# Two attention layers on one core: the rows of an image to come are transposed and measured one pass earlier and kept in DRAM

## The chip, the cores and the metric

The kernel runs on one core of a Trainium2 chip (the NeuronCore has TensorE for matrix products, VectorE, ScalarE and GpSimd for elementwise work, and SyncE, here called SP, which issues most DMAs). The metric is the time of one execution on the device in microseconds; lower is better. In the profile the engines are called PE (TensorE products), PEld (TensorE weight loads), DVE (VectorE), ACT (ScalarE), POOL (GpSimd) and SP.

## What is computed

x is 8 images of 32 x 32 positions with 512 channels, all float32. Two layers follow one another, each added to its input. Both first take a group norm over 32 groups of 16 channels.

```python
# layer 0: 16 heads of 32
x = x + L0(gn(x))     # qkv = xn @ w_qkv; softmax(q k^T * 32**-0.5) v; @ w_proj + b_proj
# layer 1: 4 heads of 128, with relative position logits
x = x + L1(gn(x))     # scores = (xn @ Wq * 128**-0.5) k^T + pos(q); softmax(scores) v; @ Wo

def _gn(v, G=32, eps=1e-5):
    g = v.reshape(B, H, W, G, C // G)
    m = mean(g, axis=(1, 2, 4)); s = var(g, axis=(1, 2, 4))
    return (g - m) / sqrt(s + eps)
```

`pos(q)` is a sum of a term by columns and a term by rows of the image; both come from products of q with two small tables.

## The kernel before

**Data.** An image is 1024 rows (positions) of 512 channels. The kernel works on it turned over, channels on the 128 partitions in CC = 4 chunks, 1024 positions along a row, so that one image is one "block" of 128 x 4 x 1024 float32 (2 MB). There are BLOCKS = 8 such blocks in SBUF. A projection is done as seven products of quarter matrices in place of eight (`seven`, L461; the sums that this needs are formed on VectorE by `forming`, L397, the operations at L424: four additions or subtractions of 128 x 1024, of which the second is wanted by the second product of a unit, and the last, called s4, by the sixth). The seven products of a unit run in the order 0, 5, 1, 4, 6, 2, 3 into three PSUM banks called x, y and z in the profile; products 5, 4 and 2 go to y. After product 5 VectorE makes a = y + p1 (L475), after product 4 b = y + p1 (L483), and the next product into y has to wait for that read.

**Passes.** The main loop (L1481) goes over b = 0 to 8. Pass b runs, on PE, the first attention of image b (`attention_0`, L766). Between its steps `side_by_side` (L1395) puts the rest of the work, in this order: the output projection of the first attention of image b-1 (`after_0`), the output projection of the second attention of image b-2 (`after_1`) woven with the second group norm of image b-1 (`norm_1`, `sums_1`), the projections of the second layer of image b-1 (`second`), the second attention of image b-1 (`attention_1`, L961), and the three projections of the first layer of image b+1 (`before_0`). The second attention counts nothing in that planning, so that all its steps stand together: it is a stage of its own of some 110 to 125 us. Images 0 and 1 are loaded in other ways; from image 2 on `load_apart` does it.

**First attention.** A step computes scores for four heads of 32 (L779), one exponential of 128 x 2048 on ScalarE (L794, tile e_room), four products with the values (L805), and one addition of 128 x 2048 on VectorE (L817, e_room) for the sum of the softmax. There are three e_room buffers, one of which holds the sum, and a single scores tile in PSUM. So an addition that is late holds up the exponential two steps later, and that the next scores.

**Second attention.** 64 steps (4 heads, 2 halves of the queries, 8 tiles of the keys). For each step SP loads a tile of 128 x 512 position rows (pos<-pr, 256 KB, L943), one of 8 slots; GpSimd adds the columns' term to it (L948), some four steps ahead; ScalarE copies it into PSUM (L957); PE adds the scores to it (L998); ScalarE takes the exponential (L1001); PE multiplies with the values (L1012); VectorE adds up e (L1026, L1028). A new slot is loaded when the copy has read it.

**The load of an image (`load_apart`, L1122).** It is woven into the second attention (L1545), three calls in every eight steps. For each of 8 parts (chunk cc, half h) `load_blocks` (L289) issues four DMAs of 64 KB on SP into a tile xs of tag "row", in pieces of 32 channels (128 B), up to three parts ahead. VectorE turns xs over into the block (L1135), `statistics` (L299) takes bn_stats of both halves of a chunk (L306) and an aggregate (L307), and SP puts the chunk away to DRAM (`put_away`, L275) for the addition of the residual later. Then `group_norm` (L312) runs: some ten small VectorE operations on 32 columns, a reciprocal root on GpSimd (rstd, L350, held behind the newest of GpSimd's position additions), four tensor_scalar of 128 x 1024 that write the block in place (L354), and the sums of `forming`.

**Tag "row".** Three buffers of 128 x 512. xs tiles use them, and so do the tiles ot of `put_out` (L1344), into which VectorE turns the output over before four DMAs of 64 KB bring it out (L1355).

**Weights.** `Stream` (L199) loads each weight tile (L235, L231) seven products ahead into one of 16 buffers, all on SP. In the second attention it holds back seven loads and releases one per step from step 6 on (L1072).

**What sets the order.** The kernel is written against a framework that schedules each engine's instructions from their dependencies and buffers and may move an instruction ahead of earlier ones of the program; `tc.issue_after(x)` keeps an instruction behind x. Each engine and SP's queue then runs its instructions strictly in the order given. A DMA on SP that waits (for a transpose, or a free buffer) holds up all DMAs behind it.

Of the kernel before, what the change touches and what calls it, by code (L numbers as in the profile page):

```python
# [27 lines left out]
def quick_path(  # L28
# [260 lines left out]
    def load_blocks(b, cc, h):  # L289

        xs = mem.tile([P, NB // 32, 32], F32, tag="row", name=f"xs_{b}_{cc}_{h}", bufs=3)
        for a in range(P // 32):
            nc.sync.dma_start(
                xs[32 * a : 32 * a + 32],
                by_blocks(xf[b, h * NB : (h + 1) * NB, :], cc * P + 32 * a),
            )
        return xs.rearrange("p t i -> p (t i)")

    def statistics(st, xT, cc, name):  # L299

        if "mv" not in st:
            st["mv"] = mvs[0]
            mvs.reverse()
        s = small.tile([P, NH, 6], F32, tag="st", name=f"st_{name}_{cc}", bufs=2)
        for h in range(NH):
            nc.vector.bn_stats(s[:, h, :], xT[cc][:, h * NB : (h + 1) * NB])  # L306
        nc.vector.bn_aggr(  # L307
            st["mv"][:, : 2 * CC].rearrange("p (s c) -> p c s", c=CC)[:, cc, :],
            s.rearrange("p h s -> p (h s)"),
        )  # L310

    def group_norm(st, xT, name, after=None, behind=None, out=None, apart=False):  # L312
# [33 lines left out]
        if apart:  # L346
            yield 0
        rstd = small.tile([P, CC], F32, tag="rstd", name=f"rstd_{name}")
        with tc.issue_after(spread[0].ins) if apart else nullcontext():
            nc.gpsimd.tensor_tensor(rstd, var, neg_half, op=ALU.pow)  # L350
        yield 0
        for cc in range(CC):
            with tc.issue_after(behind().ins) if behind is not None else nullcontext():
# [11 lines left out]

    in_place = [False]
    behind_sums = [False]
    spread = [None]

    begun = [None]  # L370
    half_done = [None]
# [513 lines left out]
    class Seeds:  # L885
# [59 lines left out]
        def add_up(self, upto):  # L945
            while self.summed < min(upto + 1, H1 * NH * NT):
                i = self.summed
                spread[0] = nc.gpsimd.tensor_tensor(  # L948
                    self.rows[i], self.rows[i], self.columns[i // NT], op=ALU.add
                )  # L950
                self.summed += 1
# [9 lines left out]
    def attention_1(q, k, v, seeds, b, beside=0, final=False):  # L961
# [93 lines left out]
        for i, at in enumerate(steps):  # L1055
            for t in range(i, i + 1 if i < beside else i + 2):
                prepare(t)
            e = front(i, *at)
            for t in range(i + 2, i + 1 if i < beside else i + AHEAD):
                prepare(t)  # L1060
            if pending is not None:
                back(*pending)
            pending = (*at, e)
            for part in ending:
                next(part, None)
            if "ended" in state:
                ending = [finish(*state.pop("ended"))]
                next(ending[0], None)
            if i + 1 < beside:
                prepare(i + 1)  # L1070
            if i > 5:
                stream.release()  # L1072
            stream.behind = seeds.last
            yield 0
# [14 lines left out]
    def load(b, st):  # L1089
# [2 lines left out]
        parts = [(cc, h) for cc in range(CC) for h in range(NH)]  # L1092

        if b > 1:
            yield from load_apart(b, st, parts)
# [23 lines left out]
        for _ in range(2):  # L1119
            yield next(sums)  # L1120

    def load_apart(b, st, parts):  # L1122

        def bring(i):
            with tc.issue_after(stream.behind.ins):
                return load_blocks(b, *parts[i])

        ahead = [bring(i) for i in range(3)]
        yield 0
        x = block(f"x0T_{b}")  # L1130
        xT = chunks(x)
        st["kept"] = []
        for i, (cc, h) in enumerate(parts):
            with tc.issue_after(added[0].ins):
                nc.vector.transpose(xT[cc][:, h * NB : (h + 1) * NB], ahead.pop(0))  # L1135
            if h == NH - 1:
                statistics(st, xT, cc, f"0_{b}")
                st["kept"] += put_away(xT[cc : cc + 1], f"0_{b}_{cc}")
            yield 0
            if i + 3 < len(parts):  # L1140
                ahead.append(bring(i + 3))
        late, later_on = lambda: added[0], lambda: begun[0]
        yield from group_norm(st, xT, f"0_{b}", after=late, behind=late, apart=True)
        fs = st["xn"] = []
        sums = st["sums0"] = forming(x, f"xn0_{b}", behind=(late, late, late, later_on), into=fs)
        for _ in range(3):
            yield next(sums)
# [268 lines left out]
    def chain(*parts):  # L1416
        for part in parts:
            yield from part
# [11 lines left out]
    def later(part, *args):  # L1430

        yield from part(*args)
# [48 lines left out]
    for b in range(B + 1):  # L1481
# [14 lines left out]
        if last is not None:  # L1496
# [21 lines left out]
                total += PRODUCT // 2  # L1518
            rest.append(later(second, b - 1, last))
            total += SECOND  # L1520
            if past is not None and coming is not None:

                total -= 1
# [18 lines left out]
            if here is None:  # L1542
                incoming = later(late_output, past)
            if here is not None and coming is not None:
                rest.append(woven(attention, incoming, 3, 8, (0, 3, 4)))  # L1545
            else:
                rest.append(woven(attention, incoming, 4, 5))
        else:
# [509 lines left out]
```

## Time and profile before

Three runs took 3718.1, 3721.3 and 3730.5 us.

| | |
|---|---|
| median of the runs | 3721.3 us |
| time of the profiled execution | 3727.5 us |
| span of its instructions | 3725.6 us |
| mean granted TensorE clock | 0.995 |
| second attentions with a load beside them (six) | 122.6, 120.0, 119.4, 122.1, 118.5, 123.8 us |
| second attention of the last image (nothing loaded beside it) | 109.5 us |
| 8 transposes and 8 bn_stats of a load | 703 and 690 ns each |
| an xs DMA (64 KB) from issue to landing | 1.9 / 3.8 / 10.2 us (least, median, most) |
| a fetch of 512 KB in whole rows (x1T<-d) | 6.0 us (median) |
| DMA over the span | 419.4 MB, 113 GB/s |

Times are in us unless ns is written. In a line of a group the number after "x" is the count, then come the busy time, the mean of one in ns, and the idle time of the engine before them with what ended it. In the timeline the columns are start, duration, engine, line, operation, what is written and read, the count, and in square brackets the idle time before with its releaser. In a table of windows each engine's column is its busy time in that window. A wait line gives the total, the number of times and the longest.

### The profile page before, as it was taken

The page shows a single profiled execution, that of the slowest core. Times are in us where ns is not written, and L with a number is a line of the kernel's source. Part 1 is how long each engine was busy: PE and PEld are TensorE (multiplying, and loading weights), DVE is VectorE, ACT ScalarE, POOL GpSimd, SP SyncE. Part 2 cuts the span into 40 slices and gives each one's busy share as a digit, 9 for nine tenths or more (in the row PEclk, how much of TensorE's full clock was granted, in tenths as well). Part 3 has the DMA queues.
Part 4 walks back from the last instruction along what each step waited for, and adds up shares of the span by engine and source line. Part 5 has one row for each costly group of instructions (what it writes and reads, how often), then busy time and mean ns, then how long its engine had stood idle before and what let it go on. Part 6 is the DMA issues. An engine that isn't in the chain of part 4 may idle for free.

```text
span 3725.6 us, 81264 instructions
## 1 busy us (share of the span) xinstructions
PE 3657.9 (98%) x33992; PEld 1241.7 (33%) x33998; DVE 2571.9 (69%) x2905; ACT 2000.7 (54%) x2281; POOL 1295.9 (35%) x833
## 2 busy tenths in 40 slices
PE   9999999999999999999999999999999999999998
PEld 4232243222433234332333323333233332333343
DVE  6778667686675856769567695766857669567546
ACT  2555655546554465544655446554565545656254
POOL 1342146131551315513164131731327213166255
PEclk9999999999999999999999999999999999999999
DMA  5122175142842327423383333723337233334376
GB/s 182 62 84 92 41 179 145 48 119 56 189 138 87 89 63 193 120 95 89 80 192 96 94 89 99 190 79 100 85 96 197 73 99 78 93 105 146 93 201 144
DMA packets 575159, 419.41 MB, mean 113 GB/s; under 512 B 279840, under 2 KB 471616, under 8 KB 573760
## 3 DMA queue, kind: packets, MB, share of 16 engines
q1 hardware_dynamic: 563152, 398.33, 40.0%
q0 software_dynamic: 2608, 13.70, 1.0%
q8 instruction: 270, 4.42, 0.5%
q10 hardware_dynamic: 9024, 2.10, 0.3%
q14 instruction: 105, 0.86, 0.1%
HBM read 321.72 MB, written 92.27 MB: 111 GB/s over the span
## 4 chain that ended last, share of the span: by engine, by line
PE 90%; DMA 3%; DVE 2%; POOL 2%; ACT 1%; issue 1%; SPq 0%; ACTq 0%; DVEq 0%; POOLq 0%
PE ps L779 14%; PE acc L805 13%; PE ps L998 10%; PE acc L1012 9%; PE y_v L385 5%; PE y_q L385 4%; PE y_k L385 4%; PE x_v L385 3%; PE z_v L385 3%; PE z_q L385 3%; PE x_k L385 3%; PE x_q L385 3%; DMA pos<-pr 3%; PE z_k L385 3%; PE y_wp L385 2%; PE y_wo L385 2%
## 5 line engine op out<-in xcount | busy, mean ns | idle before, releaser
L817 DVE TENSOR_TENSOR e_room<-e_room 128x2048 f32<-128x2048 f32 x448 | 1077.6, 2405 | 446.4 <-ACT e_room L794 444.6
L794 ACT ACTIVATE e_room<-ps 128x2048 f32<-128x2048 f32 x512 | 961.9, 1879 | 745.2 <-PE ps L779 708.3
L948 POOL TENSOR_TENSOR pos<-pos,columns 128x512 f32<-128x512 f32 x448 | 655.8, 1486 | 246.5 <-DMA pos<-pr 245.4
L779 PE MATMUL ps<-q,k 32*64 32x512 f32 x8192 | 592.5, 613 | 1.0 <-ACT e_room L794 1.0
L998 PE MATMUL ps<-q,k 128*128 128x512 f32 x1024 | 538.6, 609 | 22.9 <-ACT ps L957 22.1
L1012 PE MATMUL acc<-e,v 128*128 128x512 f32 x1024 | 529.5, 600 | 17.9 <-ACT e L1001 17.9
L805 PE MATMUL acc<-e_room,v 128*32 128x512 f32 x4096 | 546.8, 604 | 0.1
L1001 ACT ACTIVATE e<-ps 128x512 f32<-128x512 f32 x512 | 305.5, 597 | 318.7 <-PE ps L998 278.9
L1028 DVE TENSOR_TENSOR es<-es,e 128x512 f32<-128x512 f32 x384 | 277.5, 723 | 194.8 <-ACT e L1001 186.7
L957 ACT COPY ps<-pos 128x512 f32<-128x512 f32 x448 | 264.7, 592 | 82.9 <-POOL pos L948 70.7
L760 POOL TENSOR_TENSOR q<-q,su 128x512 f32<-128x512 f32 x64 | 106.7, 1667 | 554.2 <-DVE su L756 550.6
L1012 PEld LDWEIGHTS acc<-e,v 128*128 128x128 f32 x1024 | 192.8, 191 | 274.0 <-issue 140.8
L998 PEld LDWEIGHTS ps<-q,k 128*128 128x128 f32 x1024 | 185.0, 191 | 269.5 <-issue 175.7
L779 PEld LDWEIGHTS ps<-q,k 32*64 32x64 f32 x8192 | 122.9, 129 | 390.3 <-issue 211.7
L805 PEld LDWEIGHTS acc<-e_room,v 128*32 128x32 f32 x4096 | 81.4, 108 | 411.2 <-issue 363.3
L644 POOL TENSOR_TENSOR k<-b_k,p_k 128x512 f32<-128x512 f32 x32 | 48.0, 1499 | 479.3 <-ACT p_k L489 479.2
L644 POOL TENSOR_TENSOR q<-b_q,p_q 128x512 f32<-128x512 f32 x32 | 60.2, 1882 | 348.4 <-ACT p_q L489 333.9
L644 POOL TENSOR_TENSOR v<-b_v,p_v 128x512 f32<-128x512 f32 x32 | 55.5, 1734 | 352.5 <-ACT p_v L489 349.6
L877 ACT COPY pos<-pp 32x512 f32<-32x512 f32 x128 | 104.2, 814 | 29.2 <-PE pp L868 28.0
L721 DVE STREAM_TRANSPOSE tu<-su 128x512 f32<-128x512 f32 x64 | 45.2, 706 | 89.0 <-ACT su L719 88.9
L1026 DVE TENSOR_TENSOR es<-e,e 128x512 f32<-128x512 f32 x64 | 69.0, 1078 | 41.8 <-ACT e L1001 41.8
L385 PE MATMUL y_q<-f_xn,w_q 128*32 128x512 f32 x768 | 91.3, 593 | 0.8 <-DVE a_q L475 0.6
(228 smaller groups left out, 4572.3 us busy)
## 6 DMA issues: line engine op xcount, KB each, us to landing
pos<-pr SPq DMA_DIRECT2D x448, 256.0 KB, 3.9
w_qkv<-ws_qkv SPq DMA_DIRECT2D x168, 128.0 KB, 2.7
d<-x0T SPq DMA_DIRECT2D x32, 512.0 KB, 4.4
x1T<-d SPq DMA_DIRECT2D x32, 512.0 KB, 6.0
d<-x1T SPq DMA_DIRECT2D x32, 512.0 KB, 3.6
pc<-pos SPq DMA_DIRECT2D x32, 512.0 KB, 6.5
pr<-pos SPq DMA_DIRECT2D x32, 512.0 KB, 7.8
columns<-pc SPq DMA_DIRECT2D x64, 256.0 KB, 5.2
```

The source lines that it names most:

```text
L385: ins = nc.tensor.matmul(out[columns, :], weights[:, columns], moving, start=start, stop=stop, skip_group_check=open_sum,)
L644: nc.gpsimd.tensor_tensor(self.dst[1][1], s(b), s(p7), op=ALU.add)
L779: nc.tensor.matmul(ps[some, r, :], k[m][rows, j * P + 64 * i : j * P + 64 * i + 64], q[m][rows, h * NB : (h + 1) * NB], start=True, stop=True,
L794: exps[0] = nc.scalar.activation(e, ps, AF.Exp, scale=D0 ** -0.5)
L805: nc.tensor.matmul(acc[r * D0 : (r + 1) * D0, :], v[:, j, c0 : c0 + D0], e[:, r, :], start=(j == blocks[0]), stop=(j == blocks[-1]),)
L817: summed[0] = nc.vector.tensor_add(state["esum"], state["esum"], e)
L948: spread[0] = nc.gpsimd.tensor_tensor(self.rows[i], self.rows[i], self.columns[i // NT], op=ALU.add)
L957: self.copied = nc.scalar.copy(ps, rows)
L998: scored[0] = nc.tensor.matmul(ps, k[h][:, keys], q[:, h, queries], start=False, stop=True, skip_group_check=True)
L1001: exps[0] = nc.scalar.activation(e, ps, AF.Exp, scale=1.0 / math.sqrt(D1))
L1012: nc.tensor.matmul(acc, v[:, j, h * D1 : (h + 1) * D1], e, start=(j == 0), stop=(j == NT - 1),)
L1028: added[0] = nc.vector.tensor_add(state["esum"], state["esum"], e)
```

## The change

The work of `load_apart` is divided into two. `turn_ahead(b + 1)` is new. It is woven into the work of pass b ahead of the second attention (that is, beside the first attention of image b), one of its ten calls every six steps of that work. It loads the parts as before, one part ahead, but turns each over into another tile of tag "row" (xt), takes bn_stats of it, and lets SP put that half away to DRAM (256 KB, so eight stores and not four). After the eighth part it runs the small operations of the group norm and the reciprocal root. Its transposes have no `issue_after`, so that dependencies and the three buffers alone say where they stand.

`load_apart`, still beside the second attention, now takes a free block, loads its four chunks from DRAM (512 KB each, whole rows of 4 KB), norms them in place with the mean and rstd that are ready, and forms the sums. The reciprocal root is no longer held behind GpSimd's position additions. The held weights are released from step 33 on and not from step 6, and `load_apart` is called twice in every eight steps and not three times. `statistics` is now a loop over `look_at`; for the other images it does the same operations, chunk by chunk, with one buffer for a chunk's bn_stats and not two.

```diff
     def statistics(st, xT, cc, name):
 
+        for h in range(NH):
+            look_at(st, xT[cc][:, h * NB : (h + 1) * NB], cc, h, name)
+
+    def look_at(st, half, cc, h, name):
+
         if "mv" not in st:
             st["mv"] = mvs[0]
             mvs.reverse()
-        s = small.tile([P, NH, 6], F32, tag="st", name=f"st_{name}_{cc}", bufs=2)
-        for h in range(NH):
-            nc.vector.bn_stats(s[:, h, :], xT[cc][:, h * NB : (h + 1) * NB])
+        if h == 0:
+            st["st"] = small.tile([P, NH, 6], F32, tag=f"st{name[0]}", name=f"st_{name}_{cc}", bufs=1)
+        s = st["st"]
+        nc.vector.bn_stats(s[:, h, :], half)
+        if h < NH - 1:
+            return
         nc.vector.bn_aggr(
...
         rstd = small.tile([P, CC], F32, tag="rstd", name=f"rstd_{name}")
-        with tc.issue_after(spread[0].ins) if apart else nullcontext():
-            nc.gpsimd.tensor_tensor(rstd, var, neg_half, op=ALU.pow)
+        nc.gpsimd.tensor_tensor(rstd, var, neg_half, op=ALU.pow)
...
-            if i > 5:
+            if i > 4 * NT:
                 stream.release()
...
-    def load_apart(b, st, parts):
-
-        def bring(i):
+    def turn_ahead(b, st):
+
+        parts = [(cc, h) for cc in range(CC) for h in range(NH)]
+        ahead = [load_blocks(b, *parts[0])]
+        st["kept"] = [
+            dram.tile([P, N], F32, tag="kept", name=f"d_0_{b}_{cc}", bufs=4 * CC) for cc in range(CC)
+        ]
+        for i, (cc, h) in enumerate(parts):
+            if i + 1 < len(parts):
+                ahead.append(load_blocks(b, *parts[i + 1]))
+            t = mem.tile([P, NB], F32, tag="row", name=f"xt_{b}_{cc}_{h}", bufs=3)
+            nc.vector.transpose(t, ahead.pop(0))
+            look_at(st, t, cc, h, f"0_{b}")
+            nc.sync.dma_start(st["kept"][cc][:, h * NB : (h + 1) * NB], t)
+            yield 0
+        st["x0"] = []
+        st["norm0"] = group_norm(st, st["x0"], f"0_{b}", behind=lambda: added[0], apart=True)
+        for _ in range(2):
+            yield next(st["norm0"])
+
+    def load_apart(b, st):
+
+        x = block(f"x0T_{b}")
+        st["x0"].extend(chunks(x))
+        for kept, xT in zip(st["kept"], st["x0"]):
             with tc.issue_after(stream.behind.ins):
-                return load_blocks(b, *parts[i])
-
-        ahead = [bring(i) for i in range(3)]
-        yield 0
-        x = block(f"x0T_{b}")
-        xT = chunks(x)
-        st["kept"] = []
-        for i, (cc, h) in enumerate(parts):
-            with tc.issue_after(added[0].ins):
-                nc.vector.transpose(xT[cc][:, h * NB : (h + 1) * NB], ahead.pop(0))
-            if h == NH - 1:
-                statistics(st, xT, cc, f"0_{b}")
-                st["kept"] += put_away(xT[cc : cc + 1], f"0_{b}_{cc}")
+                nc.sync.dma_start(xT, kept)
             yield 0
-            if i + 3 < len(parts):
-                ahead.append(bring(i + 3))
+        yield from st.pop("norm0")
         late, later_on = lambda: added[0], lambda: begun[0]
-        yield from group_norm(st, xT, f"0_{b}", after=late, behind=late, apart=True)
         fs = st["xn"] = []
...
             rest.append(later(second, b - 1, last))
             total += SECOND
+            if coming is not None:
+                rest = [woven(chain(*rest), later(turn_ahead, b + 1, coming), 3, 6)]
...
-                rest.append(woven(attention, incoming, 3, 8, (0, 3, 4)))
+                rest.append(woven(attention, incoming, 3, 8, (0, 4)))
```

More of the change, by code (lines that the diff above doesn't have):

```diff
@@ L367, in quick_path @@
     behind_sums = [False]
-    spread = [None]
     begun = [None]
@@ L947, in add_up @@
                 i = self.summed
-                spread[0] = nc.gpsimd.tensor_tensor(
+                nc.gpsimd.tensor_tensor(
                     self.rows[i], self.rows[i], self.columns[i // NT], op=ALU.add
@@ L1094, in load @@
         if b > 1:
-            yield from load_apart(b, st, parts)
+            yield from load_apart(b, st)
             return
```

## The prediction

> **What bounds the kernel now.** First the page: busy time and the chain that ended last.
>
> ```profile
> PE 3657.9 (98%) x33992; PEld 1241.7 (33%) x33998; DVE 2571.9 (69%) x2905; ACT 2000.7 (54%) x2281; POOL 1295.9 (35%) x833
> ...
> PE 90%; DMA 3%; DVE 2%; POOL 2%; ACT 1%; issue 1%; SPq 0%; ACTq 0%; DVEq 0%; POOLq 0%
> ```
>
> TensorE is the bound, so only its own stalls can be won. Second, what PE waited for:
>
> ```profile
> PE ps L998 <- ACT ps L957: 22.1, 22, 2.3
> PE acc L1012 <- ACT e L1001: 17.9, 9, 3.0
> ```
>
> 40.0 us (22 and 9 times, longest 2.3 and 3.0), all in the second attention. Third, the eight second attentions, each window cut from its first score matmul to its last (columns: width, PE, PEld, DVE, ACT, POOL busy, granted clock, DMA share, GB/s; the one at 3280 shares PE with a first attention and is left out):
>
> ```profile
> 510.17:632.75 122.58, 114.65 (x273) 49.05 (x273) 87.45 (x140) 71.96 (x132) 81.18 (x59) 0.99 0.75 185
> 973.19:1093.18 119.99, 114.16 (x274) 49.34 (x274) 91.04 (x142) 72.27 (x133) 84.99 (x61) 0.99 0.74 189
> 1428.68:1548.03 119.35, 113.32 (x275) 48.45 (x275) 89.62 (x142) 72.38 (x133) 85.19 (x61) 1.00 0.73 190
> 1883.53:2005.61 122.08, 114.73 (x274) 49.23 (x274) 90.45 (x142) 72.34 (x133) 85.96 (x61) 0.99 0.74 185
> 2341.11:2459.60 118.49, 112.58 (x275) 48.60 (x274) 90.92 (x142) 72.03 (x133) 85.06 (x61) 1.00 0.75 191
> 2795.10:2918.85 123.75, 116.55 (x276) 49.73 (x275) 89.93 (x142) 72.39 (x133) 83.21 (x61) 0.97 0.70 183
> 3576.21:3685.69 109.48, 109.48 (x269) 49.28 (x266) 68.06 (x113) 71.41 (x132) 79.00 (x61) 1.00 0.84 219
> ```
>
> The first six load the next x beside themselves. The last does not, and never stalls, though it moves more (219 GB/s). The six sum to 726.2 us; six of 109.5 are 656.9; each of the six also holds about 0.88 us of first-attention matmuls. So 726.2 - 656.9 - 5.3 = **64 us** is what the loading costs.
>
> Fourth, inside 2795: VectorE stood for the reciprocal root that GpSimd had behind its additions, and PE behind VectorE.
>
> ```profile
> 2864.57 1.75 DVE L354 TENSOR_SCALAR x0T<-x0T,back,rstd 128x1024 f32<-128x1024 f32 x1 [4.40 <-POOL rstd L350]
> ```
> ```profile
> 2863.02 1.13 PE L998 MATMUL ps<-q,k 128*128 128x512 f32 x2 [1.12 <-ACT ps L957]
> ...
> 2868.74 2.07 PE L1012 MATMUL acc<-e,v 128*128 128x512 f32 x2 [2.88 <-ACT e L1001]
> ```
>
> The same place (steps 40 to 44 of 64) loses 2.7 to 6.5 us in each of the six, 28 us in all. The rest is lost earlier, while 32 xs loads and 4 stores stand between the position rows on SP.
>
> [...] 64 KB of xs (128 B pieces) land in 3.8 us, 256 KB of position rows in 3.9. [...] the window at 2795 has a mean clock of 0.97, and 0.67 between 2865 and 2875, after the 2.88 us stall.
>
> **The change part by part.**
>
> *Leaves the six attentions:* 32 xs issues of 0.49 us on SP (2.1 MB in 128 B pieces), 4 stores of 0.5 MB that wait on SP for statistics, 8 transposes (0.70) and 8 bn_stats (0.69), 4 aggregates (0.21), the chain of nine small VectorE operations (2.5), the reciprocal root (1.0 here) and the wait for it. *Comes:* 4 loads of 0.5 MB in whole rows. They stand at SP between position rows of steps 3 to 17, need a block that the last values product freed, and are wanted from 33 us into the window; fetches of this size landed in 6.0 us. The window then moves 22.6 - 2.1 = 20.5 MB, in larger pieces, where the last window moved 24.0 (219 GB/s x 109.5 us) with no stall. Seven weight loads (0.54 us of SP each) go from step 6 on to step 33 on; PE wants them after step 64, some 50 us later. Value: nearly all of the 64. I leave 0.5 us per window for the four large loads: **-61**. Bounds: all 64; or only the norm's place, 28.
>
> *Added to the first attention:* nothing holds the new transposes back but three row buffers, so the scheduler puts them early: three halves of image b+2 already in pass b, the other five around the query projection of the next pass. There VectorE is full:
>
> ```profile
> 1760.62 2.24 DVE L817 TENSOR_TENSOR e_room<-e_room 128x2048 f32<-128x2048 f32 x1
> 1762.79 0.67 DVE L475 TENSOR_TENSOR a_q<-y_q,p_q 128x512 f32<-128x512 f32 x1
> 1763.39 2.27 DVE L817 TENSOR_TENSOR e_room<-e_room 128x2048 f32<-128x2048 f32 x1
> 1766.51 2.29 DVE L817 TENSOR_TENSOR e_room<-e_room 128x2048 f32<-128x2048 f32 x1 [0.85 <-ACT e_room L794]
> 1768.72 0.69 DVE L483 TENSOR_TENSOR b_q<-y_q,p_q 128x512 f32<-128x512 f32 x1
> 1769.32 1.22 DVE L424 TENSOR_TENSOR f_xn<-x1T,f_xn 128x1024 f32<-128x1024 f32 x1
> ```
> ```profile
> 1770.78 1.90 PE L385 MATMUL y_q<-f_xn,w_q 128*32 128x512 f32 x16
> ```
>
> Passes 2 to 6: one half with its aggregate (1.6 us) goes in at 1745, the next (1.4) between the additions of 1763 and 1766. Delay at 1766: 1.6 - 0.85 idle + 1.4 = 2.1. The last sum f_xn then ends at 1770.5 + 2.1 = 1772.6, and the product that reads it, at 1770.78, starts 1.9 late. Behind it VectorE has idle time (56 of 100 us busy from 1770), which takes the other halves and the small chain. 5 x 1.9 = **+9.5**. Bounds: 0 to 3 us each (two halves and their aggregate all exposed, with nothing below zero: no work leaves this stretch).
>
> Pass 1 has no output stage, and its order packs five halves and the chain into 356 to 381, then three halves of the next image:
>
> ```profile
> 374.47 4.67 DVE L817 TENSOR_TENSOR e_room<-e_room 128x2048 f32<-128x2048 f32 x2
> ...
> 381.39 4.68 DVE L817 TENSOR_TENSOR e_room<-e_room 128x2048 f32<-128x2048 f32 x2
> 385.99 0.68 DVE L475 TENSOR_TENSOR a_q<-y_q,p_q 128x512 f32<-128x512 f32 x1
> ```
> ```profile
> 386.73 1.92 PE L385 MATMUL y_q<-f_xn,w_q 128*32 128x512 f32 x16
> ```
>
> Ahead of that a_q stand 1.6 + 1.4 + 1.6 + 1.4 + 0.7 (halves), 3.4 (the last half with its chain and aggregate) less some 0.5 idle: 9.6 us. It frees the bank that the product at 386.73 writes, so it ends at 396.3 and PE waits 9.6. With a landing that is awaited or a half clock after so long a stall: **+11.5** (6 to 14). In pass 0 three halves of 1.5 meet little slack: **+1** (0 to 4). At the start the statistics now go chunk by chunk, and the second half's copy is awaited one bn_stats earlier: **+1**.
>
> *SP there:* per image 32 xs issues, 8 stores instead of 4, each waiting for its transpose with the weights queued behind it. In pass 3 the unit that PE begins at 1776 has its third weight issued at 1747; now it follows the outputs (to 1764), four xs (2 us) and a store that waits till about 1769: out near 1770, landed 2.4 later, wanted at 1781.7. 9 us to spare: nothing; if that cover fails, PE waits for every weight behind it. The outputs' row buffers, three before, are now two at times; their transposes come as the 2 us landings end: nothing. GpSimd's reciprocal root (1 to 2 us) moves to where GpSimd has some 14 of 100 us busy: nothing. Four matmuls (0.88 us) move from inside each attention to after it: nothing.
>
> Sum: -61 + 9.5 + 11.5 + 1 + 1 = **-38**. The profiled execution took 3727.5 (span 3725.6); 3727.5 - 38 = 3689.5. The median of the three is 6.2 lower, 3721.3: **3683**.
>
> **The rivals.** *A, VectorE's slack hides the moved work* (additions up to 5 us late are borne today): loss about 3, so 3721 - 61 + 3 = 3663. Against: product and last sum are 0.25 us apart at 1770. 0.15. *B, the position stream stays late*: 512 KB loads among rows wanted every 1.7 us; only the norm's 28 is won, 23 is lost: 3716. Against: the last window. 0.14. *C, slower: the three row buffers.* VectorE stands for an xs group whose issue waited on SP for a store, which waited for VectorE: a group issued late costs 4 x 0.49 + 3.8 = 5.8 us. It decides from 38/48 = 0.8 us at each of the 48 halves; with 1.5 more, 48 x 1.5 = 72: 3755. Against: each group is issued some 5 us ahead of its transpose in the order. 0.08. The order was read from the built program, so that the work moves at all is not in doubt.
>
> **How the numbers follow.** Forecast 0.63 (own range 3670 to 3702). Measurement of this kernel tells 0.3%, 11 us, from no change. Faster: forecast, A and a third of B, 0.83; same: the rest of B, 0.09; slower: C, 0.08. The range 3661 to 3713 takes in A, the bounds of the terms and half of B.
>
> **What would show it.** Six attention windows of 109.5 to 111 us with no PE wait over 1 us; a PE wait of about 2 us for f_xn in the query product of passes 2 to 6, one or more summing to some 10 in pass 1; rstd gone from the attention. Wrong if PE there still waits for ACT ps behind POOL pos, or if VectorE waits for xs.

## The result, and the profile after

| | before | changed |
|---|---|---|
| median of six runs each, us | 3725.4 | 3689.3 |
| lowest and highest | 3718.1, 3730.5 | 3688.1, 3691.0 |
| profiled execution: time, span | 3727.5, 3725.6 | 3691.0, 3688.8 |

The ratio is 0.9905, with a 95% interval of 0.9892 to 0.9917: 36 us faster, where 38 were forecast. The median of before in these six runs is 4.1 us above that of the three shown ahead of the prediction. How much is won depends on the occasion: e6 below, which runs as the changed kernel does, was 30 us faster than the runs of before beside it.

Busy time and the chain that ended last, of the changed kernel:

```profile
PE 3641.0 (99%) x33992; PEld 1244.9 (34%) x33998; DVE 2547.7 (69%) x2905; ACT 1999.0 (54%) x2281; POOL 1288.6 (35%) x833
...
PE 94%; DVE 3%; DMA 1%; issue 1%; ACT 1%; POOL 0%; SPq 0%; ACTq 0%; DVEq 0%; POOLq 0%
```

TensorE is still the bound, and the share of the chain that lies on it rose from 90 to 94%. What PE waited for in the changed kernel (total, times, longest):

```profile
PE y_q L391 <- DVE f_xn L430: 9.3, 5, 2.9
PE y_q L391 <- DVE a_q L481: 5.4, 2, 4.8
PE turned L1182 <- DMA x_rows<-in_x: 5.2, 2, 5.0
PE x_v L391 <- issue: 5.0, 1, 5.0
PE y_k L391 <- DVE a_k L481: 2.4, 1, 2.4
PE sums L833 <- DVE e_room L823: 2.1, 2, 1.7
...
PE ps L1004 <- ACT ps L963: 0.5, 2, 0.3
```

The 40 us of waits for ps and e in the second attention are down to 0.5. In their place stand waits for VectorE in the projections: 9.3 us for f_xn, in five places, and 7.8 for a_q and a_k. The six second attentions with a load, and below them the last one without (width, busy time of PE, PEld, DVE, ACT and POOL, clock, DMA share, GB/s):

```profile
524.80:634.30 109.50, 109.50 (x267) 49.28 (x267) 71.66 (x112) 71.44 (x132) 76.97 (x58) 1.00 0.65 187
980.60:1090.00 109.40, 109.40 (x265) 49.23 (x266) 73.07 (x113) 71.88 (x133) 82.06 (x60) 1.00 0.63 188
1428.20:1537.70 109.50, 109.50 (x269) 49.28 (x266) 75.36 (x113) 71.95 (x133) 81.63 (x60) 1.00 0.61 187
1875.70:1985.20 109.50, 109.50 (x268) 49.28 (x266) 73.94 (x113) 71.94 (x133) 82.81 (x60) 1.00 0.63 188
2324.00:2433.50 109.50, 109.50 (x267) 49.29 (x267) 73.11 (x113) 71.92 (x133) 83.39 (x60) 1.00 0.59 187
2771.50:2881.00 109.50, 109.50 (x267) 49.29 (x267) 76.06 (x113) 71.92 (x133) 82.53 (x60) 1.00 0.63 187
3539.30:3648.80 109.50, 109.50 (x270) 49.29 (x267) 68.31 (x113) 71.46 (x132) 79.81 (x61) 1.00 0.89 219
```

All seven have one width to 0.1 us, with PE busy from end to end. Four loads in whole rows cost an attention nothing that can be seen.

**The ledger.** PE runs the same products in both kernels, and in the same order but for a few matmuls of the first attention that left each second attention (eight records in most windows), so each product of one trace can be set against the same product of the other. The shift of its start (changed minus before) says where time was won and lost:

```
                                  shift at its end   step
start (first 50 us)                     +2.4         +2.4
pass 0 (near 100)                       +4.3         +1.9
pass 1 (360 to 396)                    +14.6        +10.3
attention near 550                      +2.5        -12.1
pass 2 (near 860)                       +7.4         +4.8
attention near 1030                     -2.3         -9.6
pass 3 (near 1310)                      -0.5         +1.8
attention near 1490                     -9.5         -9.0
pass 4 (near 1765)                      -7.8         +1.6
attention near 1940                    -19.6        -11.7
pass 5 (near 2220)                     -17.1         +2.4
attention near 2400                    -25.3         -8.2
pass 6 (near 2670)                     -23.6         +1.7
attention near 2850                    -37.0        -13.4
end                                    -36.9
```

The attentions sum to -64.0, the losses to +27.0 (each step is rounded).

### The profile page after: what moved, and what is told of

Read it like the earlier page. It is cut to its first block, busy times and chain, and to the rows that moved or that the text cites. A ratio compares the mean times of both kernels' runs of the same rounds, so it can differ in the third digit from the quotient of the medians.

```text
span 3688.8 us, 81250 instructions
## 1 busy us (share of the span) xinstructions
PE 3641.0 (99%) x33992; PEld 1244.9 (34%) x33998; DVE 2547.7 (69%) x2905; ACT 1999.0 (54%) x2281; POOL 1288.6 (35%) x833
## 4 chain that ended last, share of the span: by engine, by line
PE 94%; DVE 3%; DMA 1%; issue 1%; ACT 1%; POOL 0%; SPq 0%; ACTq 0%; DVEq 0%; POOLq 0%
PE ps L785 14%; PE acc L811 13%; PE ps L1004 12%; PE acc L1018 12%; PE y_v L391 5%; PE y_k L391 4%; PE y_q L391 4%; PE x_v L391 3%; PE z_v L391 3%; PE x_k L391 3%; PE z_k L391 3%; PE z_q L391 3%; PE x_q L391 3%; PE y_wp L391 2%; PE y_wo L391 2%; PE sums L833 2%
## 5 line engine op out<-in xcount | busy, mean ns | idle before, releaser
L954 POOL TENSOR_TENSOR pos<-pos,columns 128x512 f32<-128x512 f32 x448 | 642.7, 1452 | 193.0 <-DMA pos<-pr 190.4
L1004 PE MATMUL ps<-q,k 128*128 128x512 f32 x1024 | 530.2, 600 | 0.5 <-ACT ps L963 0.5
```

The costliest lines, as they stand in the source:

```text
L954: nc.gpsimd.tensor_tensor(self.rows[i], self.rows[i], self.columns[i // NT], op=ALU.add)
L1004: scored[0] = nc.tensor.matmul(ps, k[h][:, keys], q[:, h, queries], start=False, stop=True, skip_group_check=True)
```

## The experiments

Medians in us. The kernel before had medians from 3719.4 to 3727.7 on different occasions, so each kernel's ratio to the runs of before beside it is given too. Where a smaller difference is at stake, the shift of PE between two traces is used.

| run | median | before beside it | ratio, 95% interval |
|---|---|---|---|
| e1, norm later (from before) | 3701.2 | 3727.4 | 0.9931, 0.9914 to 0.9947 |
| e2, xs in one DMA of whole rows (from before) | 3667.3 | 3727.4 | 0.9842, 0.9826 to 0.9859 |
| e3, root held again (from the change) | 3689.2 | 3727.4 | 0.9905, 0.9888 to 0.9921 |
| e4, weights released early (from the change) | 3688.4 | 3727.4 | 0.9895, 0.9879 to 0.9912 |
| e5, halves moved behind the query projection (from the change) | 3664.7 | 3719.4 | 0.9853, 0.9839 to 0.9868 |
| e6, statistics buffers (from the change) | 3689.2 | 3719.4 | 0.9923, 0.9910 to 0.9935 |
| e7, second bn_stats (from the change) | 3710.9 | 3719.4 | 0.9978, 0.9971 to 0.9984 |
| e8, e5 and e6 | 3665.4 | 3719.4 | 0.9855, 0.9840 to 0.9870 |
| e9, xs in four DMAs of whole rows (from before) | 3675.1 | 3727.7 | 0.9860, 0.9844 to 0.9877 |
| e10, pieces of 128 B beside the attention (from the change) | 3696.4 | 3727.7 | 0.9918, 0.9902 to 0.9935 |
| e11, stores later (from before) | 3706.3 | 3724.0 | 0.9945, 0.9928 to 0.9961 |

Two questions are asked of them. What made the 64 us in the attentions (e1 to e4, e9 to e11)? And what made the 27 us of losses (e5 to e8)? They are told in the order of these questions.

### e1: the norm reached five additions later

```diff
         yield 0
+        if apart:
+            yield 0
+            yield 0
         for cc in range(CC):
             with tc.issue_after(behind().ins) ...:
```

> The kernel before, with one edit: the four tensor_scalar of the norm beside the second attention are called two calls later, so VectorE reaches the first of them five additions (about 8.5 us) after the place where it stood for the reciprocal root. GpSimd's order is untouched. My theory (two causes: 28 us lie at the norm's place, steps 40 to 44, because VectorE stands behind GpSimd; 36 us lie earlier and come from the xs loads and stores among the position rows on SP): the waits of PE for e in that stretch go, the waits for ps earlier stay; 20 to 28 us less than the kernel before. Rival (everything comes from late position rows, and PE waits for them there in any case): within 5 us of the kernel before, with the PE waits of steps 40 to 44 now put down to ps behind GpSimd.

Measured: 26 us less. The six windows sum to 702.3 us, 24 less than before. PE's waits in it:

```profile
PE ps L1001 <- ACT ps L960: 23.5, 24, 2.5
...
PE acc L1015 <- ACT e L1004: 2.4, 6, 0.5
```

The wait for e fell from 17.9 to 2.4 us, and the wait for ps stayed (22.1 before). VectorE no longer waits for rstd beside the attention (19.5 us in seven places before). So what the norm's place cost was VectorE standing for GpSimd. The 20 to 28 us of my theory hold, at least as what can be had by this edit alone.

### e2 and e9: the xs parts in whole rows

e2 replaces the four DMAs of a part by one, e9 keeps four:

```diff
-                return load_blocks(b, *parts[i])
+                cc, h = parts[i]
+                xs = mem.tile([P, NB], F32, tag="row", ..., bufs=3)
+                for a in range(0, P, 32):                       # e9
+                    at = (cc * NH + h) * P + a
+                    nc.sync.dma_start(xs[a : a + 32], xf[b, at : at + 32, :])
+                return xs
```

> The kernel before, but beside the second attention each xs part is fetched by one DMA of 256 KB in whole rows of 2 KB from another place of x (the gathering of channels is left out, so other numbers are transposed and normed), in place of four DMAs of 64 KB in pieces of 128 B. Transposes, statistics, stores and the norm stay. My theory: SP spends 8 issues in place of 32 and the rows come on time; of the 36 us that lie ahead of the norm most goes, 20 to 36 us less; what stays is the wait for the reciprocal root, some of it shorter if GpSimd is no longer late. Rival (the four stores that wait on SP for statistics hold the rows up, not the xs loads): less than 10 us less.

> The kernel before, each xs part again by four DMAs of 64 KB on SP as it has them, but each of 32 whole rows of 2 KB from another place of x (the gathering of channels is left out, other numbers are transposed and normed). The run with one DMA of 256 KB in whole rows took back 60 of the 64 us; two things differ there from the kernel before, the number of issues and the size of the pieces. If the pieces of 128 B are the cause: 3665 to 3673, as with one DMA. If the 24 issues more on SP are (24 x 0.49 = 12 us of SP in each window): 3705 or more, within 20 us of the kernel before.

Measured: e2 60 us less, e9 53 us less. e2 was off my range on the good side: I had given whole rows 20 to 36 us and the norm's place the rest, but with whole rows the norm's wait went as well, although the edit touches neither VectorE's nor GpSimd's part of it. e9 took 2 us more than the upper end of what was expected of the pieces. It shows that the number of issues is a small part (8 us between e2 and e9): most of the gain comes from cutting the same 64 KB into rows of 2 KB and not into pieces of 128 B.

It is not that small pieces land late. In this stage a DMA of 64 KB lands 4.1 us after its issue in pieces of 128 B (median of 192, before) and 3.8 in whole rows (e9), and the position rows of the six windows land after 4.5 us on the mean in both. What differs is SP's time.

How 128 B pieces become stalls can be followed there. In the kernel before, part of one window:

```profile
2843.39 2.22 SPq L275 DMA_DIRECT2D d<-x0T  x1
2845.71 1.37 SPq L943 DMA_DIRECT2D pos<-pr  x2
2847.13 0.62 SPq L943 DMA_DIRECT2D columns<-pc  x1
2847.84 1.16 SPq L943 DMA_DIRECT2D pos<-pr  x2
2853.59 0.33 SPq L275 DMA_DIRECT2D d<-x0T  x1
2854.01 3.84 SPq L943 DMA_DIRECT2D pos<-pr  x6
```

The columns are start and duration of SP's issues. SP's issue of a store took 2.22 us, and from 2849.0 to 2853.6 SP stood for the next store, whose chunk VectorE turned over only by 2853.56. Behind it waited position rows, which then left six in a row. The same place of e9, where SP's order is the same:

```profile
2798.60 0.34 SPq L275 DMA_DIRECT2D d<-x0T  x1
2799.05 1.46 SPq L943 DMA_DIRECT2D pos<-pr  x2
2800.56 0.61 SPq L943 DMA_DIRECT2D columns<-pc  x1
2801.26 1.16 SPq L943 DMA_DIRECT2D pos<-pr  x2
2804.75 0.33 SPq L275 DMA_DIRECT2D d<-x0T  x1
2805.17 4.05 SPq L943 DMA_DIRECT2D pos<-pr  x6
```

The store's issue takes 0.34 us, and SP stands 2.3 us and not 4.6. Over the whole of this attention, the sixth, the 32 xs issues take 13.5 us of SP in e9 and 18.8 before, the four stores 1.4 and 5.5. Those 9.4 us are SP's, in a stretch in which every position row waits for SP.

### e3: the reciprocal root held behind GpSimd's additions again

```diff
-        for _ in range(2):
-            yield next(st["norm0"])
+        yield next(st["norm0"])
...
-        nc.gpsimd.tensor_tensor(rstd, var, neg_half, op=ALU.pow)
+        with tc.issue_after(spread[0].ins) if apart else nullcontext():
+            nc.gpsimd.tensor_tensor(rstd, var, neg_half, op=ALU.pow)
```

> The changed kernel, but the reciprocal root is again computed beside the second attention and held behind the newest of GpSimd's position additions, as the kernel before had it; all else as changed. My theory: with the position rows on time GpSimd is ahead when the root is wanted, so little comes back, 0 to 6 us over the changed kernel in the sum of the six attentions; the 28 us of the kernel before were the product of both, a late GpSimd and a VectorE standing behind it. Rival (the hold itself costs what it cost before, wherever it stands): 15 to 28 us more than the changed kernel.

Measured: no difference, and all six windows are 109.5 us. The root that cost up to 26 us before costs nothing where the position rows are on time. The rival falls. In e2 and e9, too, VectorE does not wait for the root beside the attention, though the norm is untouched there. So the wait for the root was a consequence: GpSimd was late because its rows were.

### e4: the held weights released from step 6

```diff
-            if i > 4 * NT:
+            if i > 5:
                 stream.release()
```

> The changed kernel, but the seven held weight loads are again released from step 6 of the second attention on. My theory: seven issues of 0.54 us on SP, spread over seven steps of 1.7 us each, stand between the position rows where the four large loads stand too; 0 to 1 us in each of the six attentions, 0 to 6 us in all. Rival (the later release is what made the position stream come on time): 20 us or more of the gain is lost.

Measured: no difference; the six windows are 109.5 us here too. The later release adds nothing to the gain.

### e10: the pieces of 128 B put back into the attention

```diff
-        for kept, xT in zip(st["kept"], st["x0"]):
-            with tc.issue_after(stream.behind.ins):
-                nc.sync.dma_start(xT, kept)
-            yield 0
+        for cc, xT in enumerate(st["x0"]):
+            for h in range(NH):
+                half = xT[:, h * NB : (h + 1) * NB].rearrange("p (t i) -> p t i", i=32)
+                rows = xf[b, h * NB : (h + 1) * NB, :]
+                for a in range(P // 32):
+                    with tc.issue_after(stream.behind.ins):
+                        nc.sync.dma_start(half[32 * a : 32 * a + 32], by_blocks(rows, cc * P + 32 * a))
+                yield 0
```

> The changed kernel, but the four loads of the second attention come from x itself in 32 DMAs of 64 KB in pieces of 128 B straight into the block, and not from DRAM in whole rows (the turning over is left out there, so the normed numbers are others; everything ahead of the attention stays, no row buffer, transpose, statistics or store is in the attention). If the pieces of 128 B beside the position rows cost the time: the six attentions lose 20 to 60 us again in their sum. If it was what SP waited for (a free row buffer, a store behind VectorE): within 5 us of the changed kernel.

Measured: 3696.4, 7 us more than the changed kernel, so between the two forecasts and near the second. The profiled execution took 3691.2 us; the other three took 3696 to 3698. Two windows of the profile:

```profile
1875.90:1986.60 110.70, 110.70 (x277) 49.42 (x274) 76.50 (x113) 71.91 (x133) 81.75 (x60) 1.00 0.77 186
2324.60:2435.30 110.70, 110.70 (x277) 49.42 (x274) 75.00 (x113) 71.91 (x133) 80.80 (x60) 1.00 0.73 186
```

PE is busy all through. 1.2 us more than 109.5 is eight matmuls of the first attention that lie in the window again (0.9; the prediction counted four) and 0.3 of more. That is 2 us in six attentions. In pass 4 the trace loses 3.8 us more than the changed kernel's: VectorE stood 2.83 us for an output there and not 0.79, and the stall behind it met half the clock. That the profiled execution took no longer than the changed kernel's as a whole is chance: it was 3.2 us ahead at the start, where the two programs are alike, and two stalls cost 3.0 us less because the clock was not halved behind them (see the last section). So the same 32 DMAs in the same pieces do little harm to the attention by themselves, where no store, row buffer or transpose lies between them and the position rows. They also come at a slower pace than before, two calls and not three in every eight steps; what the pace alone does was not tried.

### e11: the stores one or two calls later

```diff
             if h == NH - 1:
                 statistics(st, xT, cc, f"0_{b}")
-                st["kept"] += put_away(xT[cc : cc + 1], f"0_{b}_{cc}")
+                due.append(cc)
             yield 0
             if i + 3 < len(parts):
                 ahead.append(bring(i + 3))
+            if h == NH - 1 and len(due) > 1:
+                store()          # put_away of due.pop(0), behind the newest position row
...
+        for _ in range(2):
+            yield next(norm)
+        store()
```

> The kernel before, but each of the four stores of the turned-over chunks stands on SP behind the position rows of one or two calls later, by when VectorE has long turned the chunk; pieces of 128 B, row buffers, statistics and the norm's place stay. In its trace SP stood up to 5 us for such a store with position rows queued behind it. If SP's wait for VectorE is what makes the pieces cost so much: 15 to 40 us less than the kernel before. If it is the pieces themselves, by the longer time that SP takes to issue them: within 8 us of the kernel before.

Measured: 18 us less, as expected; the six windows sum to 709.2, 17 less than before. In the six windows SP stood 34.2 us for these stores before, and 0.6 in e11. So the stores that SP waits for are a part, with the pieces unchanged.

Taken together: the norm's place alone gives 26, the stores alone 18, whole rows alone 53 to 60. That is more than the 64 there are, so these are not three shares of a sum. They are links of one chain. The pieces take SP's time, and SP stands for stores, with position rows behind it. GpSimd gets its rows late: over the kernel it stood 245 us for them before, 217 in e11, 188 in e9, 180 in e2 and 190 in the changed kernel. So scores and exponentials are late, VectorE's additions with them, its transposes stand behind these additions, and the next store waits longer; where the norm comes, VectorE stands for GpSimd. (For xs itself VectorE did not wait in these stages before.) Cutting a link gives back 18 to 60 us; the change cuts all of them.

One end stays open. e2 and e9 keep SP's waits for stores (25.8 and 21.4 us in the six windows) and give back nearly all; e10 keeps the pieces and does so too. But e11 keeps the pieces, SP hardly waits for a store in it, and it still loses 46 of the 64 us. What else of e10 counts (no work of VectorE for the load, no store at all, the slower pace) no run takes apart. A free row buffer is the least of it: ahead of the xs issues SP stood 5.1 us in all in the six windows before.

### e5: the halves moved behind the query projection

```diff
-            nc.vector.transpose(t, ahead.pop(0))
+            with tc.issue_after(summed[0].ins):
+                nc.vector.transpose(t, ahead.pop(0))
...
-                rest = [woven(chain(*rest), later(turn_ahead, b + 1, coming), 3, 6)]
+                rest = [woven(chain(*rest), later(turn_ahead, b + 1, coming), 34, 3)]
```

> The changed kernel, but each transpose of the image to come is held behind the newest softmax addition of the first attention, and the ten calls begin 34 steps into the side work, one every three steps: all eight halves now stand behind the last sum f_xn of the query projection, where VectorE has idle time. My theory (the losses of the change, 1.9 us in pass 0, 10.4 in pass 1 and 12.4 in passes 2 to 6 by the shift of PE between the two traces, come from VectorE's order ahead of the query projection alone): these 24.6 us go, less up to 3 us at new places: 3665 to 3669 against 3689. Rival A (the loss follows the work, VectorE is late wherever the halves are put): within 8 us of the changed kernel. Rival B (xs and stores on SP late in the pass hold up the loads of the second attention, or the weights): slower than the changed kernel, PE waits for weights or in the attentions.

Measured: 3664.7, 24.5 us less than the changed kernel, and as much less than e6, which ran on the same occasion. The shift of PE against the changed kernel steps by -1.9 in pass 0, -9.9 in pass 1 and -4.8, -1.8, -1.6, -2.4 and -1.7 in passes 2 to 6: the ledger's losses, each at its place. New ones sum to 1.5. (The start, alike in both, differs by 1.6 in these two traces.) All six attentions are 109.5 us. What PE still waits for:

```profile
PE x_v L391 <- issue: 4.9, 1, 4.9
PE turned L1183 <- DMA x_rows<-in_x: 4.8, 2, 4.6
PE ps L785 <- ACT e_room L800: 1.0, 3, 0.5
PE y_q L391 <- DVE a_q L481: 1.0, 2, 0.6
```

The wait for f_xn is gone. In VectorE's timeline, here of pass 4, a half now stands right behind the last sum f_xn that the query product needs:

```profile
1741.34 1.22 DVE L430 TENSOR_TENSOR f_xn<-x1T,f_xn 128x1024 f32<-128x1024 f32 x1
1742.47 0.71 DVE L1140 STREAM_TRANSPOSE xt<-xs 128x512 f32<-128x512 f32 x1
1743.21 0.69 DVE L312 BATCH_NORM_STATS2 st<-xt 128x6 f32<-128x512 f32 x1
```

It is the fastest of the versions that do the whole work, at 0.9853 of the kernel before: against the changed kernel the work is the same, and only its place differs.

### e6 and e8: two statistics buffers at the start

```diff
-            st["st"] = small.tile([P, NH, 6], F32, tag=f"st{name[0]}", ..., bufs=1)
+            st["st"] = small.tile(
+                [P, NH, 6], F32, tag=f"st{cc % 2 if name in FIRST else name[0]}", ..., bufs=1)
```

> The changed kernel, but at the start (images 0 and 1) the statistics of odd and even chunks have a buffer each again. My theory: at the start VectorE can take the first half of another chunk while a second half is still being copied, as it did before the change; 2.4 us of the 4.3 lost by the first 110 us come back: 3687 against 3689. Rival (the order at the start was changed by something else): no difference.

> Both edits together, the halves behind the query projection and two statistics buffers at the start. My theory: the two add up, 27 us below the changed kernel: 3662 to 3666, and what is left of the ledger is the 64 us of the attentions less about 2 us. Rival: one of them covers for the other, and the sum is smaller than the parts by over 3 us.

Measured: 3689.2 and 3665.4, the same as without the edit. In the trace VectorE still takes the statistics chunk by chunk, so the edit did not bring the old order back, and the runs do not test what that order is worth. What the order does can be read: in the changed kernel VectorE takes one half and then stands 1.91 us for ScalarE's copy of the next; before, it took two and stood 0.69. In the profiles of this study the first product of the value projection starts 19.2 to 20.0 us into the span where the loading of before stands (five traces) and 20.7 to 21.7 where that of the change does (eight): 1.4 us between the means, and not 2.4. Why the order at the start changed is left open.

### e7: a second bn_stats of every half

```diff
             look_at(st, t, cc, h, f"0_{b}")
+            nc.vector.bn_stats(st["st"][:, h, :], t)
```

> The changed kernel with a second bn_stats of every half of the image to come (0.69 us of VectorE each, the result is the same numbers written again; no DMA and no buffer is added). My theory (VectorE's time ahead of the query projection is what is lost): pass 0 with three halves loses about 2 us more, pass 1 with six ahead of its last a_q about 4, passes 2 to 6 0.7 to 1.4 each for two halves, and up to 2 each on top where the wait becomes long enough for the clock to halve: 10 to 22 us more than the changed kernel. Rival (the loss comes from row buffers, landings or SP): at most 3 us more.

Measured: 3710.9, 22 us more than the changed kernel, at the top of the range. (What a halved clock cost can be seen in pass 2 of the changed kernel: 1.9 us, behind a stall of 2.93.) By the shift of PE in its trace (one of the slower executions), pass 0 loses 5.1, pass 1 3.7, passes 2 to 6 1.9, 2.9, 6.0, 3.0 and 3.0.

```profile
PE y_q L391 <- DVE f_xn L430: 17.8, 5, 4.6
PE y_q L391 <- DVE a_q L481: 6.9, 3, 5.7
...
PE sums L833 <- DVE e_room L823: 3.6, 2, 3.2
```

0.7 us of VectorE per half, with no byte and no buffer added, raises the wait for f_xn from 9.3 to 17.8. The losses follow VectorE's time in that stretch; the six attentions stay at 109.5 us.

## Why the prediction was right, point by point

| step | forecast | measured in the two traces |
|---|---|---|
| the six attentions | -61 | -64.0 |
| passes 2 to 6, query projection | +9.5 | +12.4 |
| pass 1 | +11.5 | +10.3 |
| pass 0 | +1 | +1.9 |
| start | +1 | +2.4 |
| weights and stores on SP, root on GpSimd, moved matmuls | 0 | 0 |
| sum | -38 | -37 |

The sum is nearer than its parts: the attentions gave 3 us more than forecast and the losses were 4 larger, which is luck. The 3683 us that were named were 6 too low; 4 of them come from the three runs of before from which it was counted.

The signs that were named came: windows of 109.5 us with no wait above 0.3, the waits for f_xn (1.4 to 2.9 us), no wait for rstd in the attention. One sign of being wrong came too, on a small scale and beside the first attention: VectorE waited for xs twice, 1.2 us.

**The attentions.** The reasoning from the last window was right: no residue of 0.5 us per window is left. But "28 at the norm's place, the rest from xs and stores" was read as a sum, and e1, e2, e9, e11 and e3 show that it was a chain. That did not hurt the forecast, as the change removes all of it; it would have hurt for a change of one link. For rival B I let the norm's 28 be won and the other 36 stay; e1 shows that such a case exists (26), but for another edit. The landings that the prediction puts side by side, 3.8 us for 64 KB in pieces of 128 B and 3.9 for 256 KB, are no sign of what small pieces cost: in e9 64 KB in whole rows take 3.8 us too.

**Passes 2 to 6.** The mechanism and the product were right: f_xn late for the first query product.

```profile
371.07 2.60 PE L391 MATMUL y_k<-f_xn,w_qkv 128*32 128x512 f32 x16 [2.44 <-DVE a_k L481]
...
399.83 3.42 PE L391 MATMUL y_q<-f_xn,w_q 128*32 128x512 f32 x16 [4.76 <-DVE a_q L481]
...
866.08 2.67 PE L391 MATMUL y_q<-f_xn,w_q 128*32 128x512 f32 x16 [2.93 <-DVE f_xn L430]
...
1315.46 1.92 PE L391 MATMUL y_q<-f_xn,w_q 128*32 128x512 f32 x16 [1.63 <-DVE f_xn L430]
```

In pass 3 (1315) the wait is 1.63 us, where 1.9 was forecast, but two terms of that sum were wrong and cancelled. VectorE's timeline there:

```profile
1306.98 2.26 DVE L823 TENSOR_TENSOR e_room<-e_room 128x2048 f32<-128x2048 f32 x1
1310.04 0.71 DVE L1139 STREAM_TRANSPOSE xt<-xs 128x512 f32<-128x512 f32 x1 [0.80 <-DMA out<-ot]
1310.79 0.69 DVE L312 BATCH_NORM_STATS2 st<-xt 128x6 f32<-128x512 f32 x1
1311.40 2.27 DVE L823 TENSOR_TENSOR e_room<-e_room 128x2048 f32<-128x2048 f32 x1
1313.59 0.68 DVE L489 TENSOR_TENSOR b_q<-y_q,p_q 128x512 f32<-128x512 f32 x1
1314.19 1.21 DVE L430 TENSOR_TENSOR f_xn<-x1T,f_xn 128x1024 f32<-128x1024 f32 x1
```

VectorE stood 0.80 us for the landing of an output, whose row buffer the transpose takes: "their transposes come as the 2 us landings end: nothing" was wrong. Against that, the half at 1290, counted at 1.6, cost about 0.8 (by the start of a_q behind it, less the shift of PE), since a sum f_xn near it took 1.68 us where it took 2.30 before.

In pass 2 (866) the same wait for an output was 2.28 us:

```profile
860.66 0.71 DVE L1139 STREAM_TRANSPOSE xt<-xs 128x512 f32<-128x512 f32 x1 [2.28 <-DMA out<-ot]
```

So PE waited 2.93 us, and the products behind that ran at half clock, which cost another 1.9: 4.8 in all, outside the bound of 3. The half clock was bad luck: the traces of e3, e4, e6 and e10 have the same work at this place and stalls of 2.84 to 3.65 us there, and none of them met it. This is rival C's mechanism, the row buffers, on a small scale and with the outputs in the place of the xs landings. VectorE stood for outputs five times, 5.5 us in all, and for xs landings twice, 1.2 us. The term that failed is thus the row buffers at nothing; in pass 2 it is worth 1.0 us of waiting beyond the 1.9 forecast, and about 3 with the clock.

**Pass 1.** The packed order does what the sum said, but at two places: PE waits 2.44 us for a_k in the key projection and 4.76 for a_q, and each stall is followed by products at half clock (0.79 on the mean from 369 to 377 and again from 398 to 406), 1.8 and 1.4 us. Forecast was one wait of 9.6 and 1.9 for landing or clock, an estimate. So the waits were mis-sized (7.2 us), and the clock took what was missing.

**Pass 0 and the start.** Three halves cost 1.9 us ahead of one product for sums, at the middle of what was allowed (0 to 4). Of the start's 2.4, 1.4 is what the traces of this study show between the two kinds of kernel; the remaining 1 is within what traces with the same start differ by (20.7 to 21.7).

**Rival A** (VectorE's slack hides all) falls by the 27 us of losses, and by e7: more work there is more time. **Rival C**, slower, needed 0.8 us at each of 48 halves; VectorE stood for outputs, xs and stores at nine of them, 7.4 us in all.

## What to carry to other kernels

In SP's queue, where position rows stood behind a store that waited 4.6 us in the kernel before, pieces of 128 B were cheap or dear by what stood around them: the same 32 DMAs cost up to 53 us over six attentions where stores that waited for VectorE stood among them, and about 2 us (7 by the medians) where no store, transpose or row buffer did. When several waits form such a chain, what one edit gives back is no share of the whole, so shares should not be added up or subtracted. Where work that is moved off a deadline lands is worth a look: here the same transposes lost 25 us where the scheduler put them early, and 1.5 us where they were held behind the last sum that a product waits for.

## What the runs showed of the hardware that was not expected

A stall of 2.44 us in the changed kernel was enough for products at half clock behind it, while one of 3.02 us in e3, at the place in pass 2 where 2.93 us had halved the clock in the changed kernel, was not (16 products in 1.92 us, against 2.67). In e6 even 3.65 us there was not.

In the traces of before and of the changed kernel the records of the granted clock stand whole multiples of 3.413 us apart: in the changed kernel it was halved at 372.18, 399.49 and 867.12 us, 27.31 and 467.63 us from one to the next, which is 8 and 137 times 3.413, and each time for 3.413 us. In before, between the start and the last products, it was halved three times for 3.413 us and once for 6.827. Stretches of two traces, cut at these multiples (columns as for the attentions above: width, PE's busy time first, the clock third from the end):

```profile
863.71:867.11 3.40, 1.03 (x12) 0.42 (x16) 3.37 (x5) 0.43 (x1) 2.07 (x1) 1.00 0.91 208
867.12:870.52 3.40, 3.40 (x24) 0.85 (x16) 3.22 (x4) 0.00 (x0) 0.04 (x1) 0.50 0.75 224
```
```profile
860.41:863.82 3.41, 1.57 (x24) 0.16 (x8) 3.38 (x4) 2.12 (x2) 0.00 (x0) 1.00 0.53 156
863.83:867.24 3.41, 1.61 (x16) 0.55 (x20) 3.34 (x7) 0.00 (x0) 2.13 (x1) 1.00 0.82 177
867.24:870.60 3.36, 3.36 (x40) 0.78 (x36) 3.36 (x4) 0.18 (x1) 0.00 (x0) 1.00 0.79 237
```

The first is the changed kernel: its stall of 2.93 us left PE idle for 2.4 us of one stretch, and the next ran at half clock. The second is e6: its stall of 3.65 us fell on two stretches, 1.8 us in each, and the clock stayed. In the traces of before and of the changed kernel, past the first 45 us and before the last products, PE was idle for 2.3 to 3.4 us in seven such stretches at full clock, and each was followed by one at half clock; the next longest, of 1.88 us, was not. (Matmul ends in a profile are modelled, so these times are rough.) So the clock was halved behind a stall of 2.44 us and not behind one of 3.65; in the two cut here, what differed is how the idle time fell on the stretches.

The spread between executions of one kernel goes with this clock. Of the 27 of before beside e5, the four with a mean granted clock of 0.994 took 3724 to 3730 us, and the four with 0.998 or 0.999 took 3711 to 3715.

SP's own time to issue a DMA was not constant: a store of 0.5 MB took 0.34 us of SP in the stretch of e9 above. In the six attentions of before it took up to 2.62, where the DMAs ahead of it were in pieces of 128 B, and 0.33 where they were position rows.
